# A four-layer GNN and expert kernel on one core: where an expert layer's parameters are loaded, and three smaller moves in the order of work

## The chip, the core and the metric

The kernel runs on one core of a Trainium2 chip. The core has a matrix engine (TensorE, PE in the profile), three elementwise engines (VectorE, DVE; ScalarE, ACT; GpSimd, POOL) and a queue engine (SyncE, SP), which issues most of the transfers between the device's memory and the on-chip memory. Each engine works through its own list of instructions in order and waits for the others by semaphores. The metric is the device time of one execution in microseconds (us).

## The reference

A graph of 3125 nodes with 256 features and 50,000 weighted edges goes through four layers. Each layer is a graph part and an expert part; both add to `x`, and a layer norm stands ahead of each.

```
x = x + L0_gnn(norm(x))   # weights (edge by edge) times x @ W
x = x + L0_ffn(norm(x))   # gelu expert for the better half of the tokens of a router
x = x + L1_gnn(norm(x))   # two normalised convolutions over edges and loops, relu
x = x + L1_ffn(norm(x))   # 8 experts, each token goes to two
x = x + L2_gnn(norm(x))   # the weighted product four times, W0 and W1 between
x = x + L2_ffn(norm(x))   # 8 experts, two per token, a norm of its own per expert
x = x + L3_gnn(norm(x))   # norm(gamma1, beta1), convolution, + t_emb @ tW1 + c_emb @ cW1, silu; the same again
x = x + L3_ffn(norm(x))   # 8 experts, one per token, limited capacity
```

A convolution adds up the rows of the sources of each node's edges and its own. With dense tables it is a matrix product: a 3125 x 3125 table of edge counts (or of edge weights) times `x`.

## The kernel before

**Tables.** The node dimension is padded to 3200, that is 25 tiles of 128. The kernel builds dense tables in the device's memory from the edge list: `tp` (pairs of weight and count for the first two column tiles), `tw` (weights) and `tcn` (counts). GpSimd scatters them from 391 chunks of 128 edges, one indirect store a chunk (L595): first 118 of `tp`, then 273 of `tw`, then 285 of `tcn`. The edges are sorted by destination, so a column of the table is complete when the chunks up to a certain one are stored. `gate` makes a load of table columns wait for just those stores. The counts are in `tcn`, and the first graph part that reads all of them is L1_gnn.

**Pacing.** GpSimd's stores are also held back, so that they don't run far ahead of TensorE. `paced` is a generator; each time that a stage calls `self.pace(instruction)`, the next group of stores is laid out and made to wait for that instruction. The groups of the counts are cut by `PACE_C`, offsets from the first chunk of `tcn`. The calls come after the low product, after eight high products of L0_gnn, after each of the seven chunks of the L0 expert (the instruction is the last `y` of the chunk, L1015), and twice in L1's projection.

**Order.** `blocks` writes the stages in the order in which the instructions are issued; a scheduler then orders them within the engines, and buffers of a closed pool are used again by a later one. A buffer's first user waits for the last users of what lay there. SP issues its transfers in order: one that waits holds all behind it.

**Products.** A product with a table (L256, L265) goes over seven chunks of columns, six of 512 and one of 128. Per chunk it loads tiles of five times 128 rows (1280 KB each, three in flight) and runs, for each of 25 row tiles, four matmuls: two halves of the features, each as a rounded part and a rest (`h` and `h_lo`). In front of the first chunk five single row tiles are loaded. After each chunk come 16 matmuls with the layer's weights (L345).

**Expert layers.** L1_ffn, L2_ffn and L3_ffn have a class of their own. `parameters` loads the per-expert vectors (b1, and for L2_ffn also ln_g and ln_b) as rows into `flat` (L150), transposes them on TensorE (L152) and copies the columns twice (`columns`, then L1707) into `pars`. Tokens are gathered by GpSimd (L1933, `xb`), transposed (L1957), go through two products (L1979, L1988), and the result is scattered to `L_ffn_z` (L1996). Then `x` is fetched from there (L2022).

**In L0's expert** VectorE ranks the tokens by their router weight, one step for each of 25 tiles: three counting comparisons and one for ties (L999 to L1004). The steps are taken inside `expert`, one after each output tile and one after every fourth hidden block.

**The last graph part, L3_gnn**, begins with the norm of the fetched `x` by gamma1 and beta1 (L1389, L1390), which are held in `aff`; `cond` holds the term of t_emb and c_emb, made early by `l3_conditions` (L1337 to L1345) and loaded back at L1363. Both are tiles of the pool `held`.

Of the kernel before, what the change touches and what calls it, by code (L numbers as in the profile page):

```python
# [54 lines left out]


PACE_W = (270, 296, 322, 348, 374, NC)
PACE_C = (10, 36, 60, 78, 109, 129, 149, 169, 189, 210, 221, 245, 258)


class Net:
# [262 lines left out]
    def wide(self, pool):  # L324
        return pool.tile([P, 4, D + 2], F32, tag="whole", name=self.name("whole"), bufs=1)
# [160 lines left out]
    def tables(self, pool, keep_w, keep, ordered, besides):  # L486
# [188 lines left out]
        def paced():  # L675
# [4 lines left out]
            first_c = first_chunk(LOW * P)  # L680
            at = [first_c] + [first_c + n for n in PACE_C] + [NC]
            counts(at[0], at[1], behind)
# [250 lines left out]
    def expert(self, work, fm, cw, w1, b1, func, ht, w2, take, steps):  # L933


        nc = self.nc
        hid = []
        for h in range(ht):
            ps = self.psum()[:, :cw]
            for k in range(KD):  # L940
                nc.tensor.matmul(
                    ps, lhsT=w1[:, k, h * P : (h + 1) * P], rhs=fm[:, k, :], start=k == 0, stop=k == KD - 1
                )
            t = work.tile([P, 512], F32, tag="hid", name=self.name("hid"), bufs=16)
            last = nc.scalar.activation(t[:, :cw], ps, func, bias=b1[:, h : h + 1])
            hid.append(t)
            if h % 4 == 2:
                next(steps, None)
        for i in range(cw // P):
            ps = self.psum()[:, :D]  # L950
            for h in range(ht):
                nc.tensor.matmul(
                    ps, lhsT=hid[h][:, i * P : (i + 1) * P], rhs=w2[:, h, :], start=h == 0, stop=h == ht - 1
                )
            take(i, ps)
            next(steps, None)
        return last

    def expert_weights(self, pool, w1, w2, ht, bufs=2):
# [387 lines left out]
    def l3_gnn(self, after, ordered):  # L1347
# [3 lines left out]
            self.few = self.truth(self.few_i)  # L1351
        with self.reusing("l3w", side="right") as held, self.reusing("l3g") as pool:
            wide = lambda s: held.tile([P, D], F32, name=self.name(s))
            aff = [[wide(s) for s in ("gamma", "beta")] for _ in range(2)]
            cond = [wide("cond") for _ in range(2)]

            def wanted(l):
                for s, t in zip(("gamma", "beta"), aff[l - 1]):
# [307 lines left out]
class Experts:  # L1666
# [248 lines left out]
    def rest(self, steps=None, then=None):  # L1915

        with self.net.reusing(self.name) as pool:
            self.tiles(pool, chain(steps or (), self.plan_rest()), then)
# [124 lines left out]
@with_exitstack  # L2043
def kernel(ctx: ExitStack, tc: tile.TileContext, ins, out: bass.AP):
    net = Net(ctx, tc, ins, out)
    late = ctx.enter_context(tc.tile_pool(name="late", bufs=1))
    with tc.tile_pool(name="edges", bufs=1) as pool:
        net.edges(pool)

    def blocks(ordered):  # L2050
        pool = net.reusing
        l1_ffn = net.l1_ffn(late)
        with pool("cells") as keep, pool("l1k") as l1k:
            with pool("l0k") as l0k:
                with pool("l0w") as l0w:
                    front0 = net.l0_front(l0w)
                    next(front0)
                    with pool("graph") as graph:
                        clear, fill = net.tables(graph, l0k, keep, ordered, front0)
                w = net.expert_weights(l0k, net.ins["L0_ffn_w1"], net.ins["L0_ffn_w2"], 8, 1)  # L2060
                weights = net.l1_weights(l1k)
                with pool("pars") as work:
                    l1_ffn.parameters(work)
                net.l3_conditions()
                last = net.l0_ffn(*net.l0_gnn(l0k, ordered, clear, fill), *w)
            net.l1_gnn(weights, l1_ffn.front, last, ordered)
        with pool("l2p", side="right") as part:
            l2_ffn = net.l2_ffn(late)
            with pool("pars") as work:
                l2_ffn.parameters(work)  # L2070
            h, normed = net.norm_parts("n")
            l1_ffn.rest(None, normed)
            left = net.l2_gnn(*h(), l2_ffn.front, part)
            l2_ffn.rest(left)
        front, rest = net.l3_ffn(late)
        net.l3_gnn(front, ordered)
        rest()

    with tc.If(net.truth(net.ordered_i) > 0) as arm:  # L2079
        blocks(True)  # L2080
    with arm.Else():
        blocks(False)
# [24 lines left out]
```

## Time and profile before

| | us |
|---|---|
| median of three runs | 3803.46 |
| lowest and highest | 3803.05, 3805.37 |
| the profiled execution | 3800.76 |
| its span, first to last instruction | 3798.8 |

The profile is of one further execution, whose own time stands beside its span. By the timeline the stages follow each other like this:

| stage | from | to |
|---|---|---|
| edges, tables; bound by VectorE | 0 | 245 |
| weights of L1, l3_conditions | 246 | 269 |
| L0_gnn, low product and high products | 269 | 618 |
| L0_ffn | 620 | 831 |
| L1_gnn (norm, projection, two convolutions) | 831 | 1287 |
| L1_ffn | 1300 | 1525 |
| L2_gnn | 1542 | 2680 |
| L2_ffn | 2700 | 3115 |
| L3_gnn | 3141 | 3515 |
| L3_ffn | 3515 | 3798 |

How to read the lines below. In the timeline a line has the start, the time from the first to the last of a group, the engine, the line of the kernel, the operation, `output<-input` and the number of instructions; in square brackets is the idle time of the engine ahead of it and what ended it. SPq and ACTq are the queue sides of SP and ACT, which issue transfers. A line of waits has the engine, the line and what it waited for, then the total in us, how many times, and the longest. The program's names leave the layer's number out: `in_L_ffn_b` may be that of any layer.

### The profile page before, as it was taken

To read this page: it belongs to the slowest core of one execution; us is meant where nothing else is said; L and a number is where in the kernel's file an instruction comes from. 1 tells how busy PE (TensorE), PEld (TensorE's weight loads), DVE (VectorE), ACT (ScalarE), POOL (GpSimd) and SP (SyncE) were. 2 spreads that over 40 slices of the span, in tenths; PEclk is the share of its full clock that TensorE was granted. 3 is DMA by queue.
4 is the path that set the end of the run, shared out by engine and by line. 5 is a ranking of instruction groups with operands and counts; after the bars stand their busy time and mean duration, and the time that the engine had idled before them with its cause. 6 is when DMAs were issued, how large, how long until landed. Compare 5 with 4: busy or idle time off the path is not lost. (4 is left out here: it accounts for less than half of the span.)

```text
span 3798.8 us, 45847 instructions
## 1 busy us (share of the span) xinstructions
PE 3481.4 (92%) x16848; PEld 2631.3 (69%) x16848; DVE 1324.4 (35%) x4523; ACT 789.9 (21%) x1748; POOL 1052.6 (28%) x1020
## 2 busy tenths in 40 slices
PE   5778998895999699899999999999999989999698
PEld 4557885474887599788544888444799977877344
DVE  9975628741123643300000000124521117423333
ACT  3320002121112244000000000011344435322222
POOL 5777777577000154000000000000233320000232
PEclk7769999897999899899999999999999999999799
DMA  8789650013767499743543543543444566676340
GB/s 325 283 282 314 202 175 6 1 43 110 242 226 238 143 313 297 238 152 111 183 140 109 183 153 107 198 147 127 116 109 121 163 197 237 224 254 217 92 103 24
DMA packets 430037, 655.66 MB, mean 173 GB/s; under 512 B 62929, under 2 KB 206057, under 8 KB 429804
## 3 DMA queue, kind: packets, MB, share of 16 engines
q1 hardware_dynamic: 351150, 567.87, 44.5%
q0 software_dynamic: 48560, 50.07, 5.9%
q10 hardware_dynamic: 30094, 34.70, 2.7%
q8 instruction: 135, 2.21, 0.2%
q14 instruction: 98, 0.80, 0.1%
HBM read 622.05 MB, written 128.56 MB: 198 GB/s over the span
## 5 line engine op out<-in xcount | busy, mean ns | idle before, releaser
L265 PE MATMUL ps<-tt,h 128*128 128x512 f32 (+1 forms) x2800 | 1074.6, 466 | 66.1 <-DMA tt<-tcn 39.1
L265 PEld LDWEIGHTS ps<-tt,h 128*128 128x128 f32 x2800 | 515.0, 190 | 408.6 <-issue 288.4
L1979 PEld LDWEIGHTS ps<-xe,w 128*128 128x128 f32 x2688 | 318.3, 193 | 13.5 <-issue 4.0
L1979 PE MATMUL ps<-xe,w 128*128 128x128 f32 x2688 | 322.9, 277 | 4.4 <-DVE xe L1959 2.9
L1988 PE MATMUL ps<-w,hid 128*128 128x256 f32 x1344 | 313.1, 383 | 0.3 <-ACT hid L1982 0.3
L595 POOL DMA_INDIRECT tcn<-cnt,idx_c x285 | 282.1, 990 | 108.9 <-issue 84.4
L895 PE MATMUL ps<-hw,tt 128*128 128x256 f32 x1250 | 288.1, 389 | 21.3 <-DMA tt<-tw 11.9
L305 PE MATMUL ps<-n,tt 128*128 128x256 f32 x1250 | 274.6, 383 | 16.8 <-DVE n L206 16.8
L595 POOL DMA_INDIRECT tw<-tot,idx_w x273 | 266.7, 977 | 83.2 <-issue 81.7
L895 PEld LDWEIGHTS ps<-hw,tt 128*128 128x128 f32 x1250 | 239.0, 194 | 55.5 <-issue 13.1
L305 PEld LDWEIGHTS ps<-n,tt 128*128 128x128 f32 x1250 | 240.3, 192 | 51.1 <-DVE n L206 17.6
L1247 POOL DMA_DIRECT2D L_ffn_z<-x x5 | 3.8, 764 | 978.4 <-DVE bn L1186 902.4
L305 PE MATMUL ps<-h,tt 128*128 128x256 f32 x1250 | 270.0, 379 | 0.0
L1988 PEld LDWEIGHTS ps<-w,hid 128*128 128x128 f32 x1344 | 248.8, 192 | 30.3 <-ACT hid L1982 0.5
L265 PE MATMUL ps<-tt,lo 128*128 128x512 f32 (+1 forms) x700 | 260.4, 379 | 0.0
L265 PE MATMUL ps<-tt,h_lo 128*128 128x512 f32 (+1 forms) x700 | 260.3, 379 | 0.0
L305 PEld LDWEIGHTS ps<-h,tt 128*128 128x128 f32 x1250 | 237.5, 190 | 32.3
L1982 ACT ACTIVATE hid<-ps,par 128x128 f32<-128x128 f32 x672 | 226.3, 364 | 160.4 <-PE ps L1979 124.1
L1996 POOL DMA_INDIRECT L_ffn_z<-yb,to x112 | 147.8, 1320 | 324.1 <-ACT hid L1982 216.1
L345 PE MATMUL ps<-w,fmc 128*128 128x256 f32 x700 | 171.1, 397 | 17.4 <-ACT fmc L1083 13.8
L547 DVE SCALAR_TENSOR_TENSOR eq<-cells,dinv_row,ahead 128x256 bf16<-128x256 f32 (+3 forms) x391 | 179.5, 519 | 0.0
L1140 DVE TENSOR_SCALAR h<-ps 128x256 f32<-128x256 f32 x24 | 10.2, 425 | 478.7 <-PE ps L305 478.7
(408 smaller groups left out, 3952.5 us busy)
## 6 DMA issues: line engine op xcount, KB each, us to landing
tt<-tw SPq DMA_DIRECT2D x120, 1280.0 KB
tt<-tcn SPq DMA_DIRECT2D x119, 1280.0 KB
w<-in_L_ffn_W SPq DMA_DIRECT2D x112, 1024.0 KB
w<-in_L_ffn_W SPq DMA_DIRECT2D x112, 512.0 KB
tw<-zero_row SPq DMA_DIRECT2D x23, 1600.0 KB
tt<-tw SPq DMA_DIRECT2D x36, 768.0 KB
tcn<-zero_row SPq DMA_DIRECT2D x13, 1472.0 KB
w<-in_L_ffn_w SPq DMA_DIRECT2D x18, 1024.0 KB
```

Of the source, the lines that this page charges most:

```text
L265: nc.tensor.matmul(pair[m], lhsT=part[:, k, m * P : (m + 1) * P], rhs=tt[:, j, :].bitcast(dt), start=k == 0 and i == 0, stop=k == NT - 1 a ...
L305: nc.tensor.matmul(ps[i], lhsT=tt[:, j, i * P : (i + 1) * P], rhs=h[:, k, :], start=k == 0, stop=k == NT - 1)
L345: self.nc.tensor.matmul(ps, lhsT=fm[:, k, i * P : (i + 1) * P], rhs=w[:, k, :], start=k == 0, stop=row is None and k == KD - 1)
L547: nc.vector.scalar_tensor_tensor(eqs[j], cells[k][:, at : at + m], self.col["w"][:, j : j + 1], ahead[:, GROUP * P - m :], op0=ALU.is_equa ...
L595: st = nc.gpsimd.indirect_dma_start(out=table[:, :], out_offset=bass.IndirectOffsetOnAxis(ap=idx[:, c : c + 1], axis=0), in_=src[:, c, :], ...
L895: nc.tensor.matmul(ps[:, i * D : (i + 1) * D], lhsT=tt[:, j - a, (i0 + i) * P : (i0 + i + 1) * P], rhs=hw[:, j, :], start=j == a, stop=j = ...
L1140: nc.vector.tensor_scalar(new[:, t, :], ps, 0.5, None, op0=ALU.mult)
L1247: put(dst[t0 * P : (t0 + full) * P, :].rearrange("(t p) d -> p t d", p=P), src[:, :full, :])
L1979: nc.tensor.matmul(ps, lhsT=w1[:, k, h * P : (h + 1) * P], rhs=xe[:, k, :], start=k == 0, stop=k == KD - 1)
L1982: nc.scalar.activation(hid[:, h, :], ps, func, bias=par[:, h : h + 1])
L1988: nc.tensor.matmul(ps, lhsT=hid[:, h, :], rhs=w2[:, h, :], start=h == 0, stop=h == ht - 1)
L1996: st = nc.gpsimd.indirect_dma_start(out=z[:, :], out_offset=bass.IndirectOffsetOnAxis(ap=self.to[ph][:, 0, j : j + 1], axis=0), in_=yb, in ...
```

## The change

Four edits.

- `PACE_C`, the marks of the counts, has as many entries as before, but from the fourth on they stand 22 to 35 chunks later. The fourth to the thirteenth were 78 to 258 and are 110 to 280.
- In `expert`, the call that takes one ranking step after each output tile is made only after every second one. A full chunk of L0's expert has two hidden-block steps and then two instead of four, so four in all.
- In `l3_gnn` the two tiles of `cond` are allocated ahead of the four of `aff`, and so take other addresses in the pool.
- In `blocks`, L2_ffn's object is made together with L1_ffn's, at the beginning. Its `parameters` come directly after those of L1_ffn, each with a pool `pars` of its own, ahead of `l3_conditions`, rather than after L1_gnn. With the object move the loads of its router (`wr`, L1684, and `br`, L1685).

```diff
-PACE_C = (10, 36, 60, 78, 109, 129, 149, 169, 189, 210, 221, 245, 258)
+PACE_C = (10, 36, 60, 110, 143, 163, 184, 203, 224, 244, 253, 268, 280)
...
             take(i, ps)
-            next(steps, None)
+            if i % 2 == 0:
+                next(steps, None)
         return last
...
             wide = lambda s: held.tile([P, D], F32, name=self.name(s))
+            cond = [wide("cond") for _ in range(2)]
             aff = [[wide(s) for s in ("gamma", "beta")] for _ in range(2)]
-            cond = [wide("cond") for _ in range(2)]
...
-        l1_ffn = net.l1_ffn(late)
+        l1_ffn, l2_ffn = net.l1_ffn(late), net.l2_ffn(late)
...
                 weights = net.l1_weights(l1k)
-                with pool("pars") as work:
-                    l1_ffn.parameters(work)
+                for ffn in l1_ffn, l2_ffn:
+                    with pool("pars") as work:
+                        ffn.parameters(work)
                 net.l3_conditions()
                 last = net.l0_ffn(*net.l0_gnn(l0k, ordered, clear, fill), *w)
             net.l1_gnn(weights, l1_ffn.front, last, ordered)
         with pool("l2p", side="right") as part:
-            l2_ffn = net.l2_ffn(late)
-            with pool("pars") as work:
-                l2_ffn.parameters(work)
             h, normed = net.norm_parts("n")
```

## The prediction

> **What bounds the kernel.** The profiled execution took 3800.76 us, 3798.8 of it span. I read the page's busy shares first, then the waits of TensorE, then what the queue in front of each of those waits was doing (SP's waits, the timelines), and last the table by windows. The page's chain of waits is empty here (0%), so it is no help.
>
> ```profile
> PE 3481.4 (92%) x16848; PEld 2631.3 (69%) x16848; DVE 1324.4 (35%) x4523; ACT 789.9 (21%) x1748; POOL 1052.6 (28%) x1020
> ...
> PEclk7769999897999899899999999999999999999799
> ```
>
> TensorE is busy for 92% of the span, and in the working stretches below its clock is 1.00. So the end moves only by what TensorE idles. Its waits, largest single ones in the last column (total, times, longest):
>
> ```profile
> PE ps L265 <- DMA tt<-tcn: 39.1, 5, 37.8
> PE ps L265 <- ACT h L318: 27.0, 3, 25.7
> ```
>
> The first is one stall of 37.8 us for a tile of counts in the second GNN layer, the second one of 25.7 us at the start of the last GNN layer. The reader should ask who kept the loads late. They are on SP's queue, whose waits say:
>
> ```profile
> SPq L150 <- DMA tcn<-cnt,idx_c: 47.1, 2, 35.3
> ...
> SPq L1359 <- PE ps L1988: 20.3, 1, 20.3
> ```
>
> L150 is the load of an expert parameter (`flat`), nothing to do with counts, yet it waits for the count scatters. SP's timeline shows what stands behind it:
>
> ```profile
> 829.60 53.19 SPq L256 DMA_DIRECT2D tt<-tcn  x11
> 930.15 0.56 SPq L150 DMA_DIRECT2D flat<-in_L_ffn_b  x1
> ```
>
> Eleven tile loads go out until 882.8, then nothing until 930.15. GpSimd issues its last of 285 count scatters at 924.84 (one per 1.27 us), and it lost time once:
>
> ```profile
> 722.84 0.96 POOL L595 DMA_INDIRECT tcn<-cnt,idx_c  x1 [22.34 <-DVE junk L1003]
> ```
>
> Around the stall, by windows (span, PE, PEld, DVE, ACT, POOL busy, clock, DMA share, GB/s):
>
> ```profile
> 880.00:897.00 17.00, 17.00 (x77) 14.09 (x76) 3.21 (x4) 4.29 (x7) 13.04 (x14) 1.00 0.45 145
> 897.00:935.00 38.00, 2.66 (x12) 1.85 (x10) 0.00 (x0) 0.00 (x0) 31.28 (x27) 0.57 0.08 20
> 935.00:950.00 15.00, 12.54 (x43) 10.00 (x44) 0.00 (x0) 0.00 (x0) 5.34 (x4) 0.72 0.83 301
> 950.00:970.00 20.00, 20.00 (x89) 16.52 (x88) 3.21 (x4) 4.29 (x7) 0.00 (x0) 1.00 0.68 225
> ```
>
> The second stall, in the timeline and the windows:
>
> ```profile
> 3115.58 0.35 SPq L1359 DMA_DIRECT2D gamma<-in_L_gnn_gamma  x1
> ...
> 3116.45 1.57 SPq L256 DMA_DIRECT2D tt<-tcn  x3
> 3116.83 1.55 POOL L1996 DMA_INDIRECT L_ffn_z<-yb,to  x1 [5.46 <-ACT yb L1995]
> ...
> 3125.20 0.84 ACTq L2022 DMA_DIRECT2D x<-L_ffn_z  x2
> ...
> 3133.17 0.43 DVE L1379 BATCH_NORM_STATS2 bn<-x 128x6 f32<-128x256 f32 x1 [17.16 <-DMA x<-L_ffn_z]
> ...
> 3141.29 0.79 PE L265 MATMUL ps<-tt,h 128*128 128x512 f32 x1 [25.74 <-ACT h L318]
> ```
>
> ```profile
> 3110.00:3115.00 5.00, 5.00 (x34) 4.64 (x34) 0.00 (x0) 2.14 (x7) 1.37 (x1) 1.00 0.01 0
> ...
> 3120.00:3125.00 5.00, 0.00 (x0) 0.00 (x0) 0.00 (x0) 0.00 (x0) 0.00 (x0) 0.50 1.02 373
> ```
>
> The DMA engines idle just before the stall and are full inside it: three tile loads of 1280 KB are issued 0.4 us before the last expert's scatter, which everything waits for.
>
> **What the Trainium skill says.** "DMA: Bandwidth & Descriptors", section "Anatomy of one DMA": a semaphore wait is made on the issuing sequencer before dispatch; so one waiting DMA holds all behind it, as SP's gap of 47 us shows. Same page, "Issuing engines are not separate DMA queues": DMAs of SP, ACT and GpSimd share the 16 engines and interleave. The trace agrees: the packets of the scatter at 3109.81 (engines free) end 2.4 us after its start, those of the one at 3116.83 end 7.7 us after. "TensorE: Matmul & The Clock Gate", Part 1: an idle stretch of about 3.4 us halves TensorE's clock, and as long a busy one restores it; the clocks 0.57 and 0.72 above are that.
>
> **The change, part by part.**
>
> *Third expert layer's parameters to the front.* In the changed program's SP order the three `flat` loads no longer stand among the count tiles. Each chunk's first tile load then waits only for its own chunk's scatters: the third chunk's for the 175th (722.84, the 130th, plus 45 x 1.27 is 780), the sixth's for the 285th. TensorE takes 25 steps of four matmuls and 16 of L345 per chunk, (100 + 16) x 0.227 = 26 us; from step 10 of the second chunk at 899.5 it reaches the sixth chunk near 899.5 + 14 + 4 + 3 x 26 = 996, and its load is wanted some 14 us (three tiles) earlier. The 285th is out at 924.8 even unmoved. So nothing else is late, and the DMA share of the next stretches (0.68 to 0.75) can carry the loads. The size: 897 to 950 holds 55 matmuls, at 20/89 = 0.225 us each 12.4 us of work in 53: **40.6 us** lost, of which 37.8 is the wait and the rest mostly the cold clock. Lower bound 37.
>
> The loads land in front instead. There three loads, three transposes and six small copies come between the second layer's parameters and l3_conditions. TensorE's chain there is serial (transposes at 253.57, 255.17, 256.29, first L1337 at 258.07, low product at 269.00); one more round trip of a load (issue to transposed 1.6 us there) and two DVE copies is about +2 us. A raw load of the low product is queued behind them on SP, some 8 us later than at 247. Against it, two issues of `wr` and `br` (0.85 and 1.51 us on SP, in a stage with the DMA at 1.0) go to the start, under the DVE-bound edges. The next stage has waits of 11.9 us in all for scatters that GpSimd's own pace sets, which swallow a part. I take **+1**, bounds -1 and +5.
>
> It also frees the second layer's first gather: GpSimd's L1933 waited until 1297.12 for a parameter copy, and TensorE's L1957 at 1299.98 idled 4.09 us for it. DVE's rank compares end at 1300.6 anyway, so I take **-1.3**, bounds 0 and -4.
>
> *`cond` before `aff`.* The buffer that overlaps the last expert's weights is now cond's. In the changed program gamma, beta and the three tile loads have no wait for L1988 and follow the previous bias load (3094.82): issued at 3095 to 3101, landed near 3112 at 360 GB/s (3.8 MB plus some 2 MB of weights). The wait moves to cond, behind them, wanted only after the first product. Then the last scatter and the fetch have free engines. A like hand-over with little traffic is in the trace, before the third GNN layer:
>
> ```profile
> 1528.73 0.98 POOL L1996 DMA_INDIRECT L_ffn_z<-yb,to  x1 [2.53 <-ACT yb L1995]
> 1530.85 3.32 ACTq L2022 DMA_DIRECT2D zt<-L_ffn_z  x7
> 1532.96 0.91 DVE L2038 TENSOR_TENSOR x<-x,zt 128x256 f32<-128x256 f32 x2 [5.05 <-DMA zt<-L_ffn_z]
> ```
>
> Scatter to fetch 2.1 us (8.4 in the stall), fetch to use 2.1 (8.0): 12.2 saved, and 1.8 more where DVE waited for the second tile at 3135.62; less 2, as the fetches of GpSimd now bunch. **-12**, bounds -6 (only the scatter gains) and -14. What is late next is the normalisation itself, about 6 us of DVE and ACT per first tile, and after it DVE, busy 15.00 of 15 us from 3145.
>
> *Later marks for the counts.* The gates by which scatters keep behind the work move to later scatters: that on DVE's eighth `y`, at the 130th (the line at 722.84), to the 164th, the others likewise, and none is late by the times of before. So the 22.3 us gap goes and the last scatter starts near 902.5. That matters only while a load waits for all scatters; with the first edit none does. **0**, bounds -1 and 0. GpSimd's L1089 (14.5 us) comes earlier and nobody waits for it.
>
> *Ranking four steps per chunk.* DVE's order in the first expert layer is the same in both programs, instruction for instruction, so **0**.
>
> Sum: -40.6 + 1 - 1.3 - 12 = -52.9; 3800.76 - 52.9 = 3747.9. The median of the runs lies 2.7 us above the profiled run, so 3750.6, say **3751**.
>
> **Rivals.**
> - A: the second stall shrinks by only 3 of the 12 us, because fetch and normalisation have a fixed latency or the early tile loads delay the scatters at 3102.81 and 3109.81 on which the last one follows. For: the scatter at 3099.01 waited 6.94 us for its predecessor under load. Against: 7 us of free engines between. Time 3751 + 9 = 3760, up to 3763.
> - B: the first stall goes only in part, the second-layer tiles being held by something that I haven't seen behind the `flat` loads. For: they also wait for three rotating buffers, so little is in store. Against: TensorE waits for no other tile between 850 and 1070, and the order of SP is known. Half the stall left: 3771; with A, 3783.
> - C, slower: with the idle gone TensorE's granted clock drops. From 935 to the end there are 2,860 us; 53 us are eaten at 1.9% less clock; at 2.2% less, 63 us are lost and the time is 3803.5 - 53 + 63 = 3813. For: the page's clock row falls below 9 where there is idle, so I can't see it under longer load. Against: over 970 to 1060, 90 us without a gap, the clock is 1.00.
> - D: the parameters at the front cost what they save: the low stage is 49 us long in all, so this can't reach 53 unless the scatters stop too. With the worst front, +5, the time is 3755.
>
> **Chances.** Forecast 0.68, A 0.15, B 0.10, nothing gained 0.02, C and D's extreme 0.05. The forecast's bounds give 3800.76 + 2.7 - (42 + 14 + 4 + 1) = 3742 and 3803.46 - (37 + 6 + 0 - 5) = 3765; the range of 3742 to 3767 takes in A and a little of B. Within 0.2% (7.6 us), which is about what a measurement of this kernel can tell from no change, lies 0.02; faster 0.93, slower 0.05.
>
> **What would show it.** Right: no TensorE wait for `tt<-tcn` above 2 us, a clock of 1.00 from 880 to 970, SP's loads L256 without a gap over 6 us there; the last count scatter near 902; the three tile loads before 3060 (3101 less 41), the restart wait of L265 for L318 near 13 us; L1933 no longer waiting for `pars`. Wrong: another wait of over 5 us in that stretch, a later low product (beyond 274), or a mean clock below 0.94.

## The result, and the profile after

| | before | after |
|---|---|---|
| median of four runs, us | 3804.41 | 3753.19 |
| lowest and highest, us | 3803.05, 3809.84 | 3749.16, 3757.44 |
| the profiled execution, us | 3800.76 | 3749.16 |
| its span, us | 3798.8 | 3747.4 |
| mean TensorE clock | 0.946 | 0.953 |

The ratio after to before is 0.9863, with an interval of 0.9846 to 0.988. The change makes the kernel 51 us faster.

The page after, its busy shares:

```profile
PE 3483.3 (93%) x16848; PEld 2635.7 (70%) x16848; DVE 1324.5 (35%) x4523; ACT 788.5 (21%) x1748; POOL 1055.8 (28%) x1020
```

The busy times of all engines are those of before within 5 us. The work is the same; what went is idle time of TensorE. Its waits show which, in the changed kernel's view of waits (total, times, longest):

```profile
PE ps L345 <- ACT fmc L1084: 13.8, 3, 12.7
PE ps L265 <- ACT h L318: 13.7, 2, 13.1
...
PE ps L265 <- DMA tt<-tcn: 2.6, 6, 0.7
```

The wait for count tiles was 39.1 us with one of 37.8 and is 2.6 us with a longest of 0.7. The restart of L265 for L318 was 25.7 us at its longest and is 13.1. The line of L345 is as long as before (12.7).

To see where the time came out, I matched the instructions of VectorE and ScalarE in the two traces one by one and took the difference of their starts. At a given time of before, the changed kernel stands so far behind (+) or ahead (-):

| time in before, us | stage | after minus before, us |
|---|---|---|
| 270 | start of the low product | +4.3 |
| 320 to 600 | products of the first layer | 0.0 in the middle, within 2 throughout |
| 890 | first product of L1_gnn | +0.3 |
| 955 | same, beyond the stall of before | -40.2 |
| 1060 | same, later | -38.5 |
| 1290 | end of L1_gnn | -35.3 |
| 1360 to 1400 | L1_ffn | -36.7 |
| 1600 to 3110 | L2_gnn, L2_ffn | -37.9 |
| 3141 | first product of L3_gnn | -50.6 |
| end | | -51.3 |

There are two large steps, at 890 to 955 and at 3110 to 3141, and between them a loss of 5 us and two gains of 1.1 and 1.5 us.

**The first step.** SP's timeline of the changed kernel, in the stretch where before had eleven tile loads, a silence, and a `flat`:

```profile
829.70 178.31 SPq L256 DMA_DIRECT2D tt<-tcn  x34
```

It is one group of 34 tile loads with no other line of SP between them: the parameter loads of L150 no longer stand in this queue. (Before's kernel shows why they had to wait. The sources of the count scatters, `cnt` and `idx_c`, lie in the pool `cells`, which is closed just ahead of L2_ffn's `pars`; so `flat` can take their place and must then wait for the last scatter. The addresses themselves are in no trace.) The table by windows, over the same stretch (span, PE, PEld, DVE, ACT, POOL busy, clock, DMA share, GB/s):

```profile
880.00:920.00 40.00, 39.79 (x174) 32.35 (x173) 4.50 (x6) 6.65 (x12) 34.19 (x27) 1.00 0.85 245
920.00:970.00 50.00, 50.00 (x217) 40.66 (x216) 6.42 (x8) 7.54 (x12) 0.58 (x1) 1.00 0.77 252
```

TensorE is busy for 89.8 of 90 us at a clock of 1.00. The last scatters of the counts are still going out in this stretch, as GpSimd's timeline shows:

```profile
903.54 0.97 POOL L595 DMA_INDIRECT tcn<-cnt,idx_c  x1 [0.30 <-issue]
904.82 0.97 POOL L595 DMA_INDIRECT tcn<-cnt,idx_c  x1 [0.30 <-issue]
```

The last one starts at 904.82, which is after 899.6, where before's TensorE ran dry, and yet TensorE goes on. SP's timeline between 884 and 902 shows on what:

```profile
887.35 13.12 SPq L256 DMA_DIRECT2D tt<-tcn  x3
```

The three start at 887.35, 895.44 and 900.11, all of them ahead of the last scatter; before's next tile load after 882.4 had to wait until 931.5. So the tiles that TensorE needs there don't need the last scatter, as the gates promise; only the parameter load did. Between the first two SP waits 7.7 us for a tile buffer that TensorE has still to read. TensorE loses nothing by it.

**The second step.** The timeline of the changed kernel at the hand-over from L2_ffn to L3_gnn:

```profile
3058.53 5.47 SPq L256 DMA_DIRECT2D tt<-tcn  x3
...
3079.12 1.55 POOL L1997 DMA_INDIRECT L_ffn_z<-yb,to  x1 [1.88 <-ACT yb L1996]
...
3081.88 0.84 ACTq L2023 DMA_DIRECT2D x<-L_ffn_z  x2
...
3083.99 0.43 DVE L1380 BATCH_NORM_STATS2 bn<-x 128x6 f32<-128x256 f32 x1 [5.92 <-DMA x<-L_ffn_z]
...
3090.73 0.80 PE L265 MATMUL ps<-tt,h 128*128 128x512 f32 x1 [13.12 <-ACT h L318]
```

The three tile loads are issued from 3058.53 and so 20.6 us ahead of the last scatter instead of 0.4. Scatter to fetch is 2.8 us (8.4 before), fetch to first use 2.1 (8.0 before), and TensorE's wait 13.12 (25.74 before), 12.6 less. By windows, while the tiles land and while the fetch does:

```profile
3060.00:3075.00 15.00, 15.00 (x103) 14.10 (x102) 2.12 (x6) 6.30 (x19) 3.12 (x2) 1.00 0.89 324
3079.00:3085.00 6.00, 0.00 (x0) 0.00 (x0) 0.70 (x3) 1.58 (x2) 3.96 (x5) 0.81 0.40 110
```

The DMA engines work under TensorE's last products (share 0.89) and are at 0.40 when the fetch needs them; before it was 0.01 and 1.02. The loads do get in the way of two earlier scatters, at 3068.58 and 3075.68, which wait 6.90 and 5.53 us for the one ahead of them, but the last one then waits only 1.88.

**The small steps.** In front, TensorE's timeline of the changed kernel:

```profile
260.70 3.17 PE L1338 MATMUL ps<-embw,col 128*1 128x256 f32 x8 [0.77 <-DMA embw<-in_L_gnn_tW]
...
271.63 1.97 PE L733 MATMUL ps<-ident,counts 128*128 128x128 f32 x8
...
324.65 5.59 PE L895 MATMUL ps<-hw,tt 128*128 128x256 f32 x17 [5.24 <-DMA tt<-tw]
```

L1337 of before started at 258.07 and starts at 260.70, and the low product 2.6 us late at 271.63. A wait for a weight tile ends at 324.65; before, the same wait ended at 323.77. By the matched starts the delay is down to 0.6 us at 320 and gone at 340. That the scatters of the weights set the end of both waits is my reading; the lines name only the tile.

Ahead of L1_ffn's first product the wait of 4.09 us for `pars` is gone. Another of 5.10 for DVE stands there (the products L1980, in the same view):

```profile
1265.75 3.79 PE L1980 MATMUL ps<-xe,w 128*128 128x128 f32 x16 [5.10 <-DVE xe L1960]
```

The net gain there is 1.5 us.

The loss of 5 us lies in L1_gnn. 1.7 us of it is spread over the first product: a chunk of counts takes 26.78 us instead of 26.46 (233.3 ns for a matmul of L265 instead of 230.0). The rest is two stretches of 3.4 us at half clock, at 1038.2 and 1219.1, which before's trace doesn't have; they cost 1.6 and 1.7 us. They can't be put down to the change: in the traces of the experiments below the first one is there in three of twelve and the second in seven, and one and the same kernel has a stretch in one execution and not in the next (the kernel with `cond` first has both on one chip and only the second on another; the changed kernel has neither when it is run again). The first of them by windows, and the 4 us ahead of it:

```profile
1034.00:1038.00 4.00, 3.07 (x24) 2.53 (x22) 0.74 (x6) 0.80 (x2) 0.00 (x0) 1.00 1.01 380
1038.00:1042.00 4.00, 3.94 (x10) 3.17 (x11) 0.72 (x2) 0.88 (x2) 0.00 (x0) 0.57 1.04 392
```

10 matmuls in the second window where 24 stood in the first, and TensorE had been idle for only 0.93 of those 4 us.

### The profile page after: what moved, and what is told of

Same layout as the page of the kernel before. It is cut to its first block, busy times and chain, and to the rows that moved or that the text cites. A ratio compares the mean times of both kernels' runs of the same rounds, so it can differ in the third digit from the quotient of the medians.

```text
span 3747.4 us, 45864 instructions
## 1 busy us (share of the span) xinstructions
PE 3483.3 (93%) x16848; PEld 2635.7 (70%) x16848; DVE 1324.5 (35%) x4523; ACT 788.5 (21%) x1748; POOL 1055.8 (28%) x1020
## 5 line engine op out<-in xcount | busy, mean ns | idle before, releaser
L265 PE MATMUL ps<-tt,h 128*128 128x512 f32 (+1 forms) x2800 | 1074.0, 466 | 16.3 <-ACT h L318 13.7
L265 PEld LDWEIGHTS ps<-tt,h 128*128 128x128 f32 x2800 | 514.5, 190 | 358.6 <-issue 288.9
L1980 PE MATMUL ps<-xe,w 128*128 128x128 f32 x2688 | 323.7, 277 | 8.2 <-DVE xe L1960 7.6
L1980 PEld LDWEIGHTS ps<-xe,w 128*128 128x128 f32 x2688 | 319.0, 193 | 17.0 <-DVE xe L1960 8.6
L305 PEld LDWEIGHTS ps<-n,tt 128*128 128x128 f32 x1250 | 240.1, 192 | 50.6 <-DVE n L206 17.3
L265 PE MATMUL ps<-tt,h_lo 128*128 128x512 f32 (+1 forms) x700 | 260.9, 380 | 0.0
L265 PE MATMUL ps<-tt,lo 128*128 128x512 f32 (+1 forms) x700 | 260.6, 380 | 0.0
L1997 POOL DMA_INDIRECT L_ffn_z<-yb,to x112 | 149.0, 1330 | 322.5 <-ACT hid L1983 201.8
L345 PE MATMUL ps<-w,fmc 128*128 128x256 f32 x700 | 172.6, 400 | 17.4 <-ACT fmc L1084 13.8
```

The source lines that it names most:

```text
L265: nc.tensor.matmul(pair[m], lhsT=part[:, k, m * P : (m + 1) * P], rhs=tt[:, j, :].bitcast(dt), start=k == 0 and i == 0, stop=k == NT - 1 a ...
L305: nc.tensor.matmul(ps[i], lhsT=tt[:, j, i * P : (i + 1) * P], rhs=h[:, k, :], start=k == 0, stop=k == NT - 1)
L345: self.nc.tensor.matmul(ps, lhsT=fm[:, k, i * P : (i + 1) * P], rhs=w[:, k, :], start=k == 0, stop=row is None and k == KD - 1)
L1980: nc.tensor.matmul(ps, lhsT=w1[:, k, h * P : (h + 1) * P], rhs=xe[:, k, :], start=k == 0, stop=k == KD - 1)
L1997: st = nc.gpsimd.indirect_dma_start(out=z[:, :], out_offset=bass.IndirectOffsetOnAxis(ap=self.to[ph][:, 0, j : j + 1], axis=0), in_=yb, in ...
```

## The experiments

They ran on three chips, called A, B and C here. On all three every kernel, the one before too, takes some 370 to 420 us longer than in the pair above, nearly all of it in the first 900 us. On which chip that pair ran isn't on record, so whether the chip makes the difference, or something else in which those executions differed, is open. I call the executions above "the pair". The first layer's products show the loss. Here is the same work of the changed kernel by windows, first in the pair (300 to 600 us), then on chip C:

```profile
300.00:600.00 300.00, 283.91 (x1643) 241.35 (x1643) 160.74 (x237) 13.91 (x30) 228.35 (x236) 0.98 0.63 205
```

```profile
473.30:972.40 499.10, 326.26 (x1643) 255.18 (x1642) 160.81 (x237) 13.82 (x30) 224.75 (x231) 0.79 0.39 123
```

The 1643 matmuls take 499 us instead of 300. The waits of the second run begin so:

```profile
PE ps L895 <- issue: 85.9, 68, 3.1
```

Before a matmul TensorE waits for nothing that the profile shows ("issue"), 68 times, at most 3.1 us each. It goes on while GpSimd's scatters stream and ends with them: from 955 us of before's time to 3110 the lag of such a run against the trace of before stays within 4 us, apart from what an edit takes out (the run with `cond` first on chip B has +373.5 at 955 and +372.7 at 3110). So these chips measure well what happens after 955, and badly what happens ahead of it.

Before's stall of 37.8 us doesn't show on them: in every kernel with the old or the later marks the lag falls by 40 us between 890 and 955, because only the trace of the pair stalls there. Its first link is there. Where the parameters are in their old place, `flat` waits for the count scatters in three runs, for 11.0 us with the old marks and for 5.0 and 9.2 us with the later ones, and goes out 5.3 to 6.3 us after the last scatter starts, as in the pair (5.3). What is missing is the loss on TensorE. Slowed by "issue", it hasn't used up its loaded tiles by then: in the run with the old marks its longest wait for a count tile is 0.9 us; with the later marks it has one of 5.3 and one of 3.7 us there, and the changed kernel on chip C, without `flat` in the queue, still one of 3.1. In the other runs with the old place SP comes to `flat` only when the scatters are over, because a tile load ahead of it is late. The expectations for chips A and B were written for a before that has the stall.

**Each part alone, chip A.** Four kernels with one edit each. Before is 4210.02 here.

```diff
-        l1_ffn = net.l1_ffn(late)
+        l1_ffn, l2_ffn = net.l1_ffn(late), net.l2_ffn(late)
...
-                with pool("pars") as work:
-                    l1_ffn.parameters(work)
+                for ffn in l1_ffn, l2_ffn:
+                    with pool("pars") as work:
+                        ffn.parameters(work)
...
-            l2_ffn = net.l2_ffn(late)
-            with pool("pars") as work:
-                l2_ffn.parameters(work)
```

> Before with one part alone: the third expert layer's object and parameters at the front; marks, ranking and cond/aff as before. My theory: the parameter loads were what held the count tiles, so the 37.8 us wait of L265 for tt<-tcn goes though the last count scatter still starts near 925: 3804.4 - 38 = 3766 (3763 to 3770), and no tile wait above 1 us. Rival (the later marks are needed too, because tiles wait for the last scatters): about 22 us of the stall stay, 3789. The stall of 25.7 us at the last graph part stays in both.

Measured 4210.05, ratio 1.0002 (0.9988 to 1.0016). The 38 us that were expected are missing, and so is the stall that they were to come from, with the parameters moved or not. Here the last scatter starts only 42.6 us after the start of the product, where before has 61.2 in the pair and the changed kernel 41.0. So this run neither shows nor refutes the theory.

```diff
+            cond = [wide("cond") for _ in range(2)]
             aff = [[wide(s) for s in ("gamma", "beta")] for _ in range(2)]
-            cond = [wide("cond") for _ in range(2)]
```

> Before with one part alone: cond allocated ahead of aff. My theory: three tile loads of 1280 KB go out before the last scatter, the stall at the start of the last graph part falls from 25.7 to about 13 us and the time by 12 to 3792 (3790 to 3794). Rival (the gain came from elsewhere or fixed latency fills the gap): the wait stays over 22 us, time 3801 or more. The first stall of 37.8 us stays in both.

Measured 4197.82, ratio 0.9965 (0.9951 to 0.9979): 14.7 us by the ratio, 12.2 by the medians. In its trace the lag against before falls by 12.1 us from 3110 to 3140, and by 0.3 to 0.9 in the kernels without this edit, on all three chips.

```diff
-PACE_C = (10, 36, 60, 78, 109, 129, 149, 169, 189, 210, 221, 245, 258)
+PACE_C = (10, 36, 60, 110, 143, 163, 184, 203, 224, 244, 253, 268, 280)
```

> Before with one part alone: the later marks for the counts. My theory: with the parameter loads still waiting for all 285 scatters, the stall follows the last scatter: it starts near 902.5, not 924.8, so the stall falls by 22.3 to about 15.5 us and the time to 3782 (3780 to 3785). Rival (the parameter loads wait for something other than the scatters): no change, 3804.

Measured 4230.66, ratio 1.0034 (1.0004 to 1.0065): a loss instead of the gain. The scatters do end earlier, the last starting 13.4 us after the start of the product, and `flat` goes with them: out at 19.7 us, where the ranking kernel below, with the old marks, has 49.3. But from 320 to 615 us of before's time, the products of the first layer, the lag grows by 204 us, and with the old marks by 157 to 163. More scatters stream beside these products, 244 instead of 212. Most of the loss comes back later, above all in the first product of L1_gnn: from 862 to 955 the lag falls by 33 us instead of 12 to 14. The kernels on chips B and C agree: with the later marks 195 to 199 us are lost in the first layer, with the others 149 to 160.

```diff
             take(i, ps)
-            next(steps, None)
+            if i % 2 == 0:
+                next(steps, None)
```

> Before with one part alone: one ranking step after every second output tile. My theory: the order of instructions on every engine is the same as before, so nothing changes: 3804, and DVE's instructions in the first expert layer start within 0.1 us of before. Rival (the edit spreads the comparisons and shortens the waits of L941 for DVE's y, 21.2 us in all): up to 5 us faster.

Measured 4212.27, ratio 0.9997 (0.9978 to 1.0015). TensorE and SP have the same instructions in the same order as before, and VectorE's differ only in where a semaphore instruction is recorded.

**Three of them on chip B, and the changed kernel with the old marks.** Before is 4177.54 here. The first three kernels are those of chip A again; the fourth is the changed kernel with `PACE_C` as it was.

> The same kernel as e1_params, once more, since in that run every engine took 400 us longer over the first 900 us and the stall in question was not there at all. Theory where the kernel before takes about 3804 and has the stall: 3766 (3763 to 3770), the wait of L265 for tt<-tcn gone although the last count scatter starts near 925. Rival: about 22 us of the stall stay, 3789.

> The same kernel as e2_cond, once more beside a kernel before of about 3804. Theory: 3792 (3790 to 3794), the stall at the start of the last graph part 13 instead of 25.7 us, the stall of 37.8 us unchanged. Rival: 3801 or more.

> The same kernel as e3_marks, once more beside a kernel before of about 3804. Theory: the stall follows the last count scatter and falls by 22.3 to about 15.5 us, time 3782 (3780 to 3785). Rival: no change, 3804.

> The changed kernel with the old marks for the counts. Theory: with the parameter loads gone nothing waits for the last scatter, which starts near 925 again; time as the changed kernel's, 3753 (3750 to 3756), all tile waits under 1 us. Rival (the marks carry part of the gain): 3760 to 3775.

| kernel | us | ratio to before | interval |
|---|---|---|---|
| parameters to the front | 4170.04 | 0.9979 | 0.9967 to 0.9991 |
| `cond` first | 4160.15 | 0.9945 | 0.9925 to 0.9965 |
| later marks | 4185.88 | 1.0021 | 1.0005 to 1.0037 |
| changed kernel, old marks | 4167.38 | 0.9974 | 0.9949 to 1.0 |

The parameters alone gain a few us here (0.1 to 0.3%), not 40. `cond` alone gains 23 us by the ratio and 17 by the medians, from four runs, and its trace again shows 12.0 of them from 3110 to 3140. The rest I can't place: single runs of one kernel on this chip lie up to 35 us apart, and the first 900 us, where they may differ, are the disturbed ones. The mechanism is in TensorE's waits, first with `cond` first, then with the parameters moved alone:

```profile
PE ps L265 <- ACT h L318: 14.6, 2, 13.7
```

```profile
PE ps L265 <- ACT h L318: 25.6, 2, 24.8
```

And in SP's: with `cond` first L1988 holds only the load of `cond` (L1363), with the old order that of gamma (L1359) and everything behind it.

```profile
SPq L1363 <- PE ps L1988: 13.6, 1, 13.6
```

```profile
SPq L1359 <- PE ps L1988: 19.5, 1, 19.5
```

The later marks cost 0.05 to 0.4% here, the second chip on which they do. With the old marks put back the changed kernel's longest wait for a count tile is 1.3 us, near the 1 us expected; its time can't be set against the changed kernel's, which didn't run on this chip.

**The last scatters held longer, chip C.** To bring the stall back on such a chip I held the last scatters longer, in before and in before with the parameters moved.

```diff
-PACE_C = (10, 36, 60, 78, 109, 129, 149, 169, 189, 210, 221, 245, 258)
+PACE_C = (10, 36, 60, 78, 109, 129, 149, 159, 164, 169, 174, 179, 184)
```

> Before, with its parameter loads in the old place, but the last marks of the counts at 159 to 184: a hundred scatters then stand behind the end of the second layer's projection and the last starts about 127 us after the first product begins (61 in before). My theory (the parameter loads hold the tiles until the last scatter has landed): TensorE stops after 10 steps of the second chunk, about 36 us into the product, until about 135 us into it, a stall of about 100 us: 60 us slower than before where that has its stall of 38, 80 to 100 slower on a chip where before has none. Rival (the tiles wait for their own chunks' scatters only): under 15 us slower.

> The same late marks, with the parameters at the front and nothing else. My theory: the last scatter is as late as in g1_late, but only the sixth chunk's tiles wait for it, wanted about 120 us into the product: a stall of 0 to 15 us, and 80 to 100 us faster than g1_late. Rival (any tile waits for all scatters): as slow as g1_late within 10 us.

Before is 4174.90 here. Measured 4211.05 without the move (ratio 1.0079, 1.0056 to 1.0103) and 4203.84 with it (1.0066, 1.0044 to 1.0087): a difference of 7 us, with intervals that overlap, where 80 to 100 were expected. The last scatter now starts 132.9 and 132.6 us after the product's start. Over the stretch in question, 862 to 955 of before's time, the lag of both grows by the same 71.8 us, so even the 7 us don't come from there. Another thing starves TensorE. The kernel with the parameters moved, by windows:

```profile
1200.00:1220.00 20.00, 20.00 (x89) 16.33 (x88) 3.06 (x5) 2.56 (x5) 12.65 (x14) 1.00 0.64 197
1220.00:1260.00 40.00, 8.36 (x27) 5.95 (x26) 1.38 (x2) 1.44 (x2) 30.55 (x32) 0.61 0.21 61
1260.00:1330.00 70.00, 18.13 (x38) 9.91 (x36) 0.00 (x0) 1.42 (x3) 53.24 (x56) 0.55 0.03 4
1345.00:1400.00 55.00, 53.61 (x225) 43.40 (x225) 8.97 (x10) 9.62 (x15) 1.51 (x2) 0.97 0.78 260
```

From 1260 to 1330 there are 38 matmuls in 70 us and next to no traffic, so no transfer is in its way. Its timeline there:

```profile
1268.66 0.19 PEld L265 LDWEIGHTS ps<-tt,h 128*128 128x128 f32 x1 [2.61 <-issue]
1270.06 0.59 PE L265 MATMUL ps<-tt,h 128*128 128x512 f32 x1 [2.40 <-issue]
1271.46 0.29 PEld L265 LDWEIGHTS ps<-tt,h_lo 128*128 128x128 f32 x1 [2.62 <-issue]
1272.87 0.59 PE L265 MATMUL ps<-tt,h_lo 128*128 128x512 f32 x1 [2.22 <-issue]
```

There is one instruction of TensorE every 1.40 us, and none waits for a tile. At 1344.96, 14.5 us after the last scatter's start at 1330.50, the matmuls are close together again. The kernel without the move shows the same picture, matmul for matmul within a few in each 10 us. SP's tile loads are themselves so late that it comes to `flat` only 171.3 us after the product's start, long after the last scatter. So these two kernels don't tell the theories apart: where the stall would be, the chip has the other shortage, with the parameter loads in the queue or without.

**The changed kernel again, and one that takes a further wait away, chip C.** In the changed kernel of the pair TensorE still waits 12.69 us ahead of L1_gnn's last products:

```profile
1251.78 2.07 PE L345 MATMUL ps<-w,fmc 128*128 128x256 f32 x4 [12.69 <-ACT fmc L1084]
```

VectorE's timeline shows what kept ScalarE from `fmc` there:

```profile
1245.33 0.18 DVE L1266 COPY lg<-ps 128x32 f32<-128x32 f32 x1 [16.78 <-issue]
1245.35 0.06 DVE L1768 MEMSET plan<- 128x3 int32 x1
```

VectorE stood still for 16.78 us. The copy L1266 had its input from TensorE at 1232.9, but ahead of it in VectorE's order is a constant for L2_ffn's plan (the two are recorded 0.02 us apart). It lies in the buffer of L1_ffn's plan and has to wait for SP's 50 reads of that (L1940), one per 0.31 us, of which the last ends at 1245.30. The edit gives L2_ffn's plan a buffer of its own:

```diff
-            [keep.tile([P, m, n], I32, tag=f"{s}_{p}", name=net.name(s)) for p, n in phases]
+            [keep.tile([P, m, n], I32, tag=f"{s}_{p}" + self.name * (m == 2), name=net.name(s)) for p, n in phases]
```

> The changed kernel, with a buffer of its own for each expert layer's plan, instead of one that the layers share. In the changed kernel DVE's constant for the third layer's plan (L1768) waits for SP's 50 reads of the second layer's plan, and TensorE's L345 for the copies behind it: 12.7 us. Theory: that wait goes and the time falls by 9 to 13 us against the changed kernel. Rival (the next thing, the gather or SP's reads, is as late): under 4 us faster.

> The changed kernel once more, on the chip of these runs. If before takes 3804 there, 3753. If the first 900 us are 400 us longer, as in the last runs, before's first stall is not there to be removed: then only the second stall's 12 us and up to 8 more are left, 0.3 to 0.5% faster.

Measured 4156.94 with it (0.9976 of before, 0.996 to 0.9993), and 4170.37 for the changed kernel (0.9985, 0.9969 to 1.0), which is at the lower end of the 0.3 to 0.5% expected or below it. So the whole change gains less here than `cond` alone did on chips A and B: of its parts only `cond` finds its stall on such chips, and the later marks cost. The wait, in the changed kernel and then with the edit, on chip C:

```profile
1669.73 2.08 PE L345 MATMUL ps<-w,fmc 128*128 128x256 f32 x4 [12.36 <-ACT fmc L1084]
```

```profile
1676.20 1.13 PE L345 MATMUL ps<-w,fmc 128*128 128x256 f32 x4 [0.65 <-ACT fmc L1084]
```

The lag against before's trace falls by 11.7 us from 1250 to 1300 with the edit and not without (399.5 to 387.8, against 382.0 to 382.3). In one profile of each that step is there, and the wait is gone as the theory said. The gain over the whole isn't settled: it is 13.4 us by the medians but 4 by the two ratios, whose intervals overlap. Whether it beats the changed kernel where that takes 3753 us wasn't tried, nor was it run with the old marks.

## Why the prediction was right

**The first stall, -40.6: measured -40.5** (from +0.3 to -40.2). The reason stands on the two traces of the pair: the silence of SP behind `flat`, gone with `flat`, and TensorE running through the last scatter on tiles loaded ahead of it. The forecast that nothing else is late there held. One sign named for it didn't come: two loads of SP stand 8.1 us apart, not at most 6, as a tile buffer was still in use. That `flat` follows the last scatter is there in three experiments, too. What the move of the parameters is worth by itself was not measured, since no chip of the experiments has this stall; the 40 us are read from two traces that differ by all four edits. These traces speak against the rival that the later marks alone would have done it. With `flat` left where it was it would have gone out 5.3 us after the last scatter, as before, so at 910.1, and TensorE restarted 7.2 us after it (930.15 to 937.4 before), at about 917: an estimate of 17 to 18 us of the stall left, of 37.8.

**What followed it was not in the sum: +5.** A slower pace in the first product (1.7) and two stretches at half clock (3.3) took back an eighth of the gain. The pace comes with the later marks, so it is a cost of the change, under a term that the sum had at nothing. The half clock comes and goes between executions of one kernel, so it need not be the change's doing. Rival C, a TensorE that runs slower once it has no pause, would have needed 63 us; the mean clock rose from 0.946 to 0.953 instead.

**The front, +1: measured +0.3 at 890.** The low product was 2.6 us late, 0.6 more than the round trip of 2 us in the working, and the waits behind it took nearly all of it, not a part.

**The gather of L1_ffn, -1.3: measured -1.5.** DVE's later work bounds it as said. Another 1.1 us came up to 1600; between the end of L1_gnn and the first products of L2_gnn the changed kernel has 48 us at half clock where before has 55, which fits, but is not shown to be the cause.

**`cond` first, -12: measured -12.7** by the matched starts (-12.6 by the wait), and -12.1 and -12.0 where it was made alone. In the changed kernel it was -12.7 on chip C, and on chip B with the old marks -8.5 (a wait of 17.2 us left in place of 13), which I can't explain from one profile. The tile loads came somewhat later than forecast: the first at 3058.5 as said (before 3060), the last 5.5 us after it. Fetch to use is the 2.1 us of the row it was taken from; scatter to fetch 2.8 instead of 2.1. Rival A, that fixed latencies keep all but 3 of the 12, falls on all of them.

**The marks, 0: nothing gained, and a small loss.** The last scatter started at 904.8 (902.5 forecast). The bounds of -1 and 0 were too kind. In the pair the slower pace of the first product costs 1.7 us. On the two chips where the marks ran alone they lose 0.2 to 0.3%, where the first layer's products are slowed; in the pair that loss isn't visible (the shift is 0.0 in the middle of 320 to 600, and 247 scatters run beside these products instead of 248).

**Ranking four steps per chunk, 0: right**, the same order of work, and 4212.27 against 4210.02 where it was made alone (ratio 0.9997, 0.9978 to 1.0015).

The sum of -52.9 stands against -51.6 in the profiled executions (-51.3 by the matched starts), 3751 against a median of 3753.19. By the table the parts are +0.3, -40.5, +4.9, -1.5, -1.1, -12.7 and -0.7 after the hand-over. So 5.0 us of loss that the sum didn't have stand against 3.4 us of gain that it took too small. The two large mechanisms were right; the agreement to 2 us is partly luck.

**Open:** the parameter move's time by itself, and why the first product has two paces. All seven kernels with the old marks run it at 230 ns for a matmul and all seven others at 233, in the pair and on every chip, so the count marks bring it, but how isn't shown. Open, too, is what makes the first 900 us of the experiments differ from the pair.

## What to carry to other kernels

Look at a stall through the queue of the engine that issues the late load, not only at the load: an unrelated transfer ahead of it (a parameter, a bias) that waits for a buffer or a store holds everything behind it, and belongs ahead of the long stage or in a buffer of its own. Where a pool reuses space, order the tiles so that the one with the late predecessor is the one wanted last, and bulk loads go out while the DMA engines are idle rather than beside a small transfer that the next stage hangs on. Test each such edit by the stage it is meant for, at matched instructions, since a whole-run ratio can hide a 12 us step behind a disturbance elsewhere.

## What was unexpected of the hardware

- On the chips of the experiments TensorE got one instruction per 1.40 us for long stretches in which GpSimd's indirect stores streamed, with the DMA share at 0.03; 14.5 us after the start of the last one it ran at full pace. In the pair the same stores at the same 1.27 us cost it nothing. A first guess is that the fetch of instructions starves. The Trainium skill, "Runtime: NRT & Kernel Launch", section "Instruction fetch mechanics", says that each sequencer fetches its instructions in blocks by a DMA queue of its own and that the cost of crossing from one block to the next is mostly hidden. The trace agrees, and speaks against the guess: between 1262 and 1345 us of the kernel with the late marks and the parameters moved there is no packet of instruction fetch at all, and the blocks ahead of it (1260.6) and after it (1365.9) took 1.06 and 1.09 us, where the changed kernel of the pair has a median of 1.02. What slows the instructions is open.
- The clock fell to half for 3.4 us after 4 us in which TensorE was busy for 3.07. The prediction cited the skill's "TensorE: Matmul & The Clock Gate", Part 1, for an idle stretch of about 3.4 us as the trigger; ahead of these two falls the longest single pause is 0.59 and 0.51 us, and each fall cost 1.6 to 1.7 us. Such pauses don't always do it: before was busy for 3.41 of 4 us at the first place (1072 to 1076) and kept its clock, and the kernel with `cond` first, as busy there on chip A, lost it.
